# Layer 3 of a four-layer graph network: bursts of five units laid out in a table of eight bursts a batch

## Chip, cores and metric

One core of a Trainium2 chip (trn2). The metric is device time in microseconds (us) of one execution. The kernel before takes 2136.28 us, the median of three runs (2132.42 to 2140.51).

## The reference

Four graph layers over `x` of 16 batches, 1024 nodes and 64 features, with one adjacency matrix of 1024 x 1024 for all. After each layer `x = layernorm(x + layer(x))`. The change touches the last layer alone:

```python
# layer 3: four heads of dimension 64, then one outer attention
mask = adj + eye(N) > 0
h = einsum('bnc,hdc->bhnd', x, Wh)
scores = where(mask, h @ h^T, -1e16)          # per batch and head, 1024 x 1024
out_h = softmax(scores) @ h + bh
z = leaky_relu(concatenate(out_h), 0.2)       # 1024 x 256
h2 = z @ Wo^T
out2 = softmax(where(mask, h2 @ h2^T, -1e16)) @ h2 + bo
z2 = leaky_relu(out2, 0.2)
out = layernorm(z2) * gamma + beta
x = layernorm(x + out)
```

## The kernel before, in words

**Work and tiles.** P = 128 partitions, C = 8 blocks of nodes, HALF = 512 columns. Layers 0 to 2 come first; the loops of layer 3 stand at lines 1606 to 1732. In layer 3 the four heads of a batch are two pairs (n = 0, 1), two heads of 64 rows in one tile of 128 partitions. The work comes in **units**. A head unit takes one block k of source nodes and one half h of the target columns, for both heads of a pair: scores on PE (L1273, four MATMULs in the trace) into a PSUM tile `s` of 128 x 1024; exp on ACT (L1277) into an SBUF tile `e`, with a per-pair bias `shift`; the 0/1 mask on DVE (L1278); and the product with the values (L1285, four MATMULs), which adds up over the eight blocks in a PSUM bank. That is 32 units a batch. An outer unit (`head_out`, 8 a batch) is the same with h2: L1370, L1375, the mask into a second tile `me` (L1377), the product L1397; the row sums are made by one more DVE instruction, `add_up` (L1388), from the unmasked `e`.

**Small tasks.** When a half of a pair is complete, ACT copies it (L1292), and `project(q)` (L1294 to L1316) multiplies it with `wb`: eight matmuls (L1302), then on DVE a copy of the sums, a reciprocal, two multiplications and `leaky` into `z`. `z_T` transposes z, `h_2T` makes h2 (PE, ACT copy and square, two DVE copies), `h_2v` its transposed values. `shift_of` (L1205) makes the bias: matmuls of squares with ones into a PSUM tile `pn`, a maximum on DVE (`top`, L1214), an all-reduce over the partitions on POOL (L1216), and `below` (L1221), a DVE instruction that is put into the list `soon`. `prep_x`, `prep_h`, `prep_sq`, `prep_v` prepare the next pair of batches. An outer result then goes through `gather`, `layer`, `mean`, `centre`, `scale`, `affine`, `residual`, `mean`, `centre`, `scale`, `finish`, nearly all on DVE; `scale` also puts a root (two small ACT instructions) into `soon`, and the root puts its three DVE steps there.

**Order.** `tc.manual_schedule` keeps PE, ACT, DVE and POOL each in the order in which the program writes. `run` (L1708) takes the units of all batches from one queue, three to a burst. Of a burst it writes: `catch_up` (all of `soon`); of each unit scores, exp and mask; the tasks in `mids`; `drain`, the products of the burst before; the tasks in `slots`; the `add_up`s. So PE makes the scores of one burst before the products of the last one. Tasks are placed by batch and by the unit's position in it (0 to 39, the outer units of the batch before at 18, 21, ...).

**Buffers.** All small tasks and scores of layer 3 share three PSUM tiles of two banks (tag `s`), taken in turn. The tiles `e`, `me` and the second load of the adjacency (`nodes_adj`, a DMA on SP's queue and a conversion on DVE) share nine SBUF tiles (tag `e`).

Of the kernel before, what the change touches and what calls it, by code (L numbers as in the profile page):

```python
# [578 lines left out]
def fast_path(  # L579
# [87 lines left out]

    soon = []
    in_order = {getattr(mybir.EngineType, e) for e in ("PE", "Activation", "DVE", "Pool")}
# [43 lines left out]
    def normalizing(y, sq, late):  # L713
# [15 lines left out]
        def scale():  # L729
            vs = small.tile([P, n], F32, tag="ln_vs", name="ln_vs")  # L730
            nc.vector.tensor_reduce(vs, sq, AX.X, ALU.add)
            ve = small.tile([P, n], F32, tag="ln_ve", name="ln_ve")
            nc.vector.tensor_scalar(ve, vs, 1.0 / D, LN_EPS, ALU.mult, ALU.add)
            rstd = small.tile([P, n], F32, tag="ln_rstd", name="ln_rstd")
            if late:
                nc.gpsimd.tensor_tensor(rstd, ve, neg_half, ALU.pow)
                return rstd
            root, step = inverse_root(rstd, ve)

            def first():  # L740
                root()
                soon.append(step)

            soon.append(first)
            return rstd
# [444 lines left out]
    def nodes_adj(c):  # L1190
        a_sb = l3.tile([P, N], I32, tag="e", name=f"adj3_{c}", bufs=9)
        nc.sync.dma_start(a_sb, adj_v[c])

        def convert():
            nc.vector.tensor_scalar(
                aN[:, c, :].rearrange("p (k q) -> p k q", q=P), a_sb.rearrange("p (q k) -> p k q", k=C),
                0.0, None, ALU.is_gt,
            )
            own = aN[:, c, c * P : (c + 1) * P]
            nc.vector.tensor_tensor(own, own, ident16, ALU.max)  # L1200

        return convert
# [61 lines left out]
    def heads(b, n):  # L1264
        held = {}

        def scores(k, h):
# [3 lines left out]
            for i in range(2):  # L1271
# [3 lines left out]
                )  # L1275
            e = l3.tile([P, 2, HALF], F32, tag="e", name="e", bufs=9)
            nc.scalar.activation(e, s, AF.Exp, bias=shifts[b, n])  # L1277
            nc.vector.tensor_tensor(e, e, bc_mid(aT[:, k, cols], 2), ALU.mult)  # L1278
            return e

        def product(k, h, e):
# [7 lines left out]
            if k == C - 1:  # L1289
                if h == 0:  # L1290
                    held["y"] = l3.tile([P, N], F32, tag="y", name=f"yT_{b}_{n}")
                nc.scalar.copy(held["y"][:, h * HALF : (h + 1) * HALF], held[h])  # L1292

        def project(q):  # L1294
# [5 lines left out]
            for j in range(CH):  # L1300
                c = q * CH + j
                nc.tensor.matmul(  # L1302
                    o[:, j // 2, j % 2, :], held["y"][:, c * P : (c + 1) * P], wb[:, n, :], start=True, stop=True,
                )
# [5 lines left out]
            for i in range(2):  # L1310
# [6 lines left out]

        units = [(lambda k=k, h=h: scores(k, h), lambda e, k=k, h=h: product(k, h, e), None)
                 for h in range(2) for k in range(C)]
        return units, project  # L1320


    def prep_out(b):
# [28 lines left out]
        def h_2v():  # L1352
            v = l3.tile([P, C, D], F32, tag="h2v", name=f"h2v_{b}", bufs=1)
            pt = one_bank("ph2v").rearrange("p (c d) -> p c d", c=C)
            for c in range(C):
                nc.tensor.transpose(pt[:, c, :], hTs[b][0][:D, c // CH, c % CH * P : (c % CH + 1) * P], ident[:D, :D])
            nc.vector.tensor_copy(v, pt)  # L1357
            vals["out", b] = v
# [3 lines left out]
    def head_out(b):  # L1362
        held = {}

        def scores(k):
            s = ps_s.tile([P, 2, HALF], F32, tag="s", name="s")
            hT = hTs[b][0]
            for i in range(2):
# [4 lines left out]
                )  # L1373
            e = l3.tile([P, 2, HALF], F32, tag="e", name="e", bufs=9)
            nc.scalar.activation(e, s, AF.Exp, bias=shifts[b])  # L1375
            m = l3.tile([P, 2, HALF], F32, tag="e", name="me", bufs=9)
            nc.vector.tensor_tensor(  # L1377
                m, e, aT[:, k, :].rearrange("p (i q) -> p i q", i=2), ALU.mult
            )
            return e, m  # L1380

        def unit(k):
            held[k], m = scores(k)
            return m

        def add_up(k):
            junk = l3.tile([P, N], BF16, tag="junk", name="junk", bufs=1)
            nc.vector.scalar_tensor_tensor(  # L1388
                junk, held.pop(k).rearrange("p i q -> p (i q)"), 1.0, aN[:, k, :], ALU.mult, ALU.mult,
                accum_out=sums[:, b, H, k : k + 1],  # L1390
            )

# [55 lines left out]
        def finish():  # L1448
# [4 lines left out]
        units = [  # L1453
            (lambda k=k: unit(k), lambda e, k=k: product(k, e), lambda k=k: add_up(k)) for k in range(C)
        ]
# [148 lines left out]


    slots, mids = {}, {}
    work = [[heads(b, n) for n in range(NP)] for b in range(B)]
    outs = [(prep_out(b), head_out(b)) for b in range(B)]
    BURST = 3
    LAST = 40  # L1610
    E = B - 1

    def at(b, p, task, where=slots):
        where.setdefault((b, p), []).append(task)

    for c in range(C):
        convert = {}
        at(0, 2 * c, lambda c=c, convert=convert: convert.update(go=nodes_adj(c)))
        at(0, 2 * c + 5, lambda convert=convert: convert["go"]())
    for b in range(B):  # L1620
# [6 lines left out]
        ends = outs[b][1][1]  # L1627
        if b < E:
            places = [13, 22, 26, 33, LAST + 4, LAST + 7, LAST + 10, LAST + 13, LAST + 14]

            end = (41, 46, 49, 55) if b < E - 2 else (29, 31, 33, 39)
            places += [2 * LAST + p for p in (6, 8, 10, 11, 14, 23, 25, *end)]
        else:
            places = [13, 22, 26, 35, *[LAST - 1] * 5, *[LAST + 8] * 11]
        if b == E - 1:
            places[9:] = [LAST + 38, *[LAST + 39] * 4, *[2 * LAST + p for p in (3, 3, 3, 3, 3, 8)]]
        for task, p in zip(chain + ends, places):
            t = min(p // LAST, max(E - b, 0))
            at(b + t, p - t * LAST, task)


    ended = slots[E, LAST - 1]
    slots[E, LAST - 1] = [ended[i] for i in (5, 0, 1, 6, 2, 3, 7, 8, 9, 4)]
    ahead = []
    for b in range(0, B, 2):
        for t, p, task, where in (
            (-1, 16, lambda b=b: prep_x(b), slots),
            (-1, 20, lambda b=b: prep_h(b, 0, 0), mids), (-1, 23, lambda b=b: prep_sq(b, 0, 0), slots),
            (-1, 26, lambda b=b: prep_h(b, 0, 1), mids), (-1, 29, lambda b=b: prep_sq(b, 0, 1), slots),
            (-1, 25, lambda b=b: prep_v(b), slots),  # L1650
            (-1, 32, lambda b=b: shift_of((b, 0), hTs[b, 0][1]), slots),
            (-1, 36, lambda b=b: shift_of((b + 1, 0), hTs[b + 1, 0][1]), slots),
            (0, 2, lambda b=b: prep_h(b, 1, 0), mids), (0, 3, lambda b=b: prep_sq(b, 1, 0), slots),
            (0, 5, lambda b=b: prep_h(b, 1, 1), mids), (0, 8, lambda b=b: prep_sq(b, 1, 1), slots),
            (0, 11, lambda b=b: shift_of((b, 1), hTs[b, 1][1]), slots),
            (0, 20, lambda b=b: shift_of((b + 1, 1), hTs[b + 1, 1][1]), slots),
            (0, 19, lambda b=b: prep_v(b + 1), slots),
        ):
            if b + t < 0:
                ahead.append(task)  # L1660
            else:
                at(b + t, p, task, where)

    with tc.tile_pool(name="ps_g", bufs=1, space=bass.MemoryType.PSUM, reuse_waits="tile") as ps_g, tc.tile_pool(
# [13 lines left out]
        ending = gat_layer(later["w2"], "l2", True, extra, first, 5, True)  # L1678
    for p, task in zip((1, 4, 7, 10, 14, 16), ending):
        at(0, p, task)  # L1680

# [16 lines left out]

    queue = []
    for b in range(B):  # L1700
        units = work[b][0][0] + work[b][1][0]
        outer = outs[b - 1][1][0] if b else [None] * C
        for i, unit in enumerate(outer):
            units.insert(18 + (3 if b < E else 2) * i, unit)
        queue += [(b, p, unit) for p, unit in enumerate(units)]
    last = [(E, LAST + p, unit) for p, unit in enumerate(outs[E][1][0])]

    def run(queue):  # L1708
        while queue:
            burst = []  # L1710
            while queue and sum(unit is not None for _, _, unit in burst) < BURST:
                burst.append(queue.pop(0))
            catch_up()
            made = [(unit[1], unit[0]()) for _, _, unit in burst if unit]
            for b, p, _ in burst:
                tasks(mids, b, p)
            drain()
            waiting.extend(lambda product=product, e=e: product(e) for product, e in made)
            if not queue:
                drain()  # L1720
            for b, p, _ in burst:
                tasks(slots, b, p)
            for _, _, unit in burst:
                if unit and unit[2]:
                    unit[2]()

    with tc.manual_schedule(engines=in_order):
        run(queue)
        run(last)
        for task in [catch_up, *slots[E, LAST + 8]]:  # L1730
            task()
            while soon:
                catch_up()

# [72 lines left out]
```

## Time and profile before

| | us |
|---|---|
| median of three runs | 2136.28 |
| the profiled execution | 2138.12 |
| its span, first to last instruction | 2136.3 |
| PE busy | 2017.2 (94%) |
| DVE busy | 1851.9 (87%) |
| ACT busy | 1227.7 (57%) |
| POOL busy | 51.2 (2%) |
| first L1273 matmul (layer 3 begins) | 695.6 |
| head exps L1277, 512 of 1.11 us | 542.5 |
| head masks L1278, 512 of 1.22 us | 602.7 |
| outer masks L1377, 128 of 1.22 us | 155.9 |
| outer sums L1388, 128 of 1.22 us | 156.0 |

The span runs from the first to the last instruction; 1.8 us of the execution lie outside it. Busy time is the union of an engine's instructions. Matmuls overlap, so their ends run into the next one: the distance of two starts tells what a matmul costs, not its duration. The same holds in a smaller measure for DVE and ACT, where the mean of 1.22 us a mask goes with 1.135 us from start to start when masks follow each other. In rows of instructions in order of time, "x12" merges neighbours of one kind, and the bracket behind gives the idle time before them and what ended it.

### The profile page before, as it was taken

How to read it: one execution, taken by the hardware profiler on the slowest of the kernel's cores; microseconds unless marked ns; L12 is line 12 of the kernel's file. 1: busy time of each engine (PE TensorE's matmuls, PEld its weight loads, DVE VectorE, ACT ScalarE, POOL GpSimd, SP SyncE). 2: the span in 40 equal slices, each digit the busy share in tenths (PEclk: the TensorE clock that was granted, in tenths of full speed). 3: DMA queues.
4: the chain of work that ended last, by engine and by line, in shares of the span. 5: the costliest groups of instructions: out<-in, count | busy, mean ns of one | idle time of the engine just before them, and what ended most of it. 6: DMA issues, size and time to landing. Idle time of an engine off the chain costs nothing.

```text
span 2136.3 us, 26123 instructions
## 1 busy us (share of the span) xinstructions
PE 2017.2 (94%) x10065; PEld 841.9 (39%) x10065; DVE 1851.9 (87%) x3224; ACT 1227.7 (57%) x1965; POOL 51.2 (2%) x77
## 2 busy tenths in 40 slices
PE   7999979999887999999999999999999999999993
PEld 3333347763332333333334333333333333333331
DVE  5888879989999868798898898889888889889997
ACT  4445556645555756556665655655655665565541
POOL 0000000000000000000000000000000000000001
PEclk9999989989999999999999999999999999999997
DMA  6000000000000100000000000000000000000000
GB/s 165 1 1 1 1 1 1 1 1 1 0 1 30 50 1 1 1 1 6 6 1 6 1 6 6 1 6 1 6 6 1 6 1 6 6 1 6 6 5 12
DMA packets 23654, 18.89 MB, mean 9 GB/s; under 512 B 19361, under 2 KB 19426, under 8 KB 23522
## 3 DMA queue, kind: packets, MB, share of 16 engines
q1 hardware_dynamic: 23218, 17.11, 2.8%
q8 instruction: 81, 1.33, 0.3%
q14 instruction: 51, 0.42, 0.1%
q10 hardware_dynamic: 304, 0.03, 0.0%
HBM read 12.95 MB, written 4.19 MB: 8 GB/s over the span
## 4 chain that ended last, share of the span: by engine, by line
PE 69%; DVE 25%; ACT 3%; issue 1%; DMA 0%; POOL 0%; SPq 0%; POOLq 0%; DVEq 0%; ACTq 0%
PE y L1285 18%; PE s L1273 17%; DVE e L964 7%; PE y_l L976 6%; PE s L1370 5%; PE y L1397 4%; DVE e L1278 4%; PE u_l L987 3%; PE po L1302 3%; PE po L1557 3%; ACT e L1277 1%; PE pg L944 1%; DVE r L1566 1%; PE pzT L1331 1%; PE ps L910 1%
## 5 line engine op out<-in xcount | busy, mean ns | idle before, releaser
L1277 ACT ACTIVATE e<-s,shift 128x1024 f32<-128x1024 f32 x512 | 542.5, 1111 | 243.1 <-PE s L1273 237.6
L1278 DVE TENSOR_TENSOR e<-e,aT 128x1024 f32<-128x1024 f32 x512 | 602.7, 1221 | 87.3 <-ACT e L1277 85.3
L1273 PE MATMUL s<-hT 64*128 64x512 f32 x2048 | 509.6, 611 | 15.5 <-DVE top L1214 8.6
L1285 PE MATMUL y<-e,vals 128*64 128x512 f32 x2048 | 490.6, 601 | 3.2 <-ACT yT L1292 1.3
L964 DVE SCALAR_TENSOR_TENSOR e<-G_l,q,aT 128x1024 f32<-128x1024 f32 x256 | 320.0, 1280 | 20.9 <-ACT G_l L945 12.8
L976 PE MATMUL y_l<-e,vals_l 128*64 128x512 f32 x1024 | 271.3, 637 | 26.5 <-DVE e L964 25.8
L1273 PEld LDWEIGHTS s<-hT 64*128 64x128 f32 x2048 | 182.4, 186 | 256.1 <-issue 170.8
L1285 PEld LDWEIGHTS y<-e,vals 128*64 128x64 f32 x2048 | 131.0, 136 | 330.6 <-issue 258.0
L1375 ACT ACTIVATE e<-s,shift 128x1024 f32<-128x1024 f32 x128 | 141.6, 1112 | 85.2 <-PE s L1370 75.0
L1377 DVE TENSOR_TENSOR me<-e,aT 128x1024 f32<-128x1024 f32 x128 | 155.9, 1221 | 16.8 <-ACT e L1375 16.5
L1388 DVE SCALAR_TENSOR_TENSOR junk<-e,aN 128x1024 bf16<-128x1024 f32 x128 | 156.0, 1219 | 0.2
L1397 PE MATMUL y<-me,h2v 128*64 128x512 f32 x512 | 135.3, 609 | 10.5 <-DVE me L1377 10.4
L1370 PE MATMUL s<-h2T 64*128 64x512 f32 x512 | 136.3, 610 | 4.6 <-DVE h2v L1357 4.4
L976 PEld LDWEIGHTS y_l<-e,vals_l 128*64 128x64 f32 x1024 | 60.7, 139 | 169.8 <-issue 57.1
L1557 PE MATMUL po<-hi,aR 128*128 128x512 f32 x256 | 102.8, 401 | 2.8 <-ACT hi L1542 1.1
L775 ACT ACTIVATE x<-m,bn_shift,bn_rstd 128x64 f32<-128x64 f32 x256 | 88.5, 430 | 23.2 <-DVE bn_shift L766 23.2
L1557 PE MATMUL po<-lo,aR 128*128 128x512 f32 x256 | 100.2, 392 | 0.0
L1332 ACT COPY zT<-pzT 128x1024 f32<-128x1024 f32 x32 | 32.4, 1013 | 78.4 <-PE pzT L1331 78.4
L1302 PEld LDWEIGHTS po<-wb,yT 128*128 128x128 f32 x512 | 62.0, 190 | 34.0 <-issue 21.1
L1302 PE MATMUL po<-wb,yT 128*128 128x130 f32 x512 | 73.8, 287 | 1.3 <-ACT e L1277 1.2
L1370 PEld LDWEIGHTS s<-h2T 64*128 64x128 f32 x512 | 46.6, 186 | 63.7 <-issue 41.3
L987 PE MATMUL u_l<-e,only 128*32 128x512 f32 x512 | 70.3, 605 | 0.0
(214 smaller groups left out, 1980.8 us busy)
## 6 DMA issues: line engine op xcount, KB each, us to landing
adj<-in_adj_dram SPq DMA_DIRECT2D x16, 512.0 KB, 4.5
x<-in_x_dram SPq DMA_DIRECT2D x16, 256.0 KB, 4.9
out_dram<-res SPq DMA_DIRECT2D x16, 256.0 KB, 2.0
wl<-in_L_gnn_Wh_dram SPq DMA_DIRECT2D x2, 64.0 KB, 3.3
wo<-in_L_gnn_Wo_dram SPq DMA_DIRECT2D x1, 64.0 KB, 3.0
l_wd<-in_L_gnn_W_dram ACTq DMA_DIRECT2D x2, 16.0 KB, 4.9
l_wd<-in_L_gnn_W_dram SPq DMA_DIRECT2D x2, 16.0 KB, 2.1
bo<-in_L_gnn_bo_dram SPq DMA_DIRECT2D x1, 32.0 KB, 3.0
```

The lines of the kernel that those rows point to most:

```text
L964: nc.vector.scalar_tensor_tensor(e, G[b - b % 2][:, b % 2, :], pq[b - b % 2][1][:, k, b % 2 : b % 2 + 1], aT[:, k, :], ALU.max, ALU.mult,)
L976: nc.tensor.matmul(held["y"][h * D : (h + 1) * D, :], vals[b][:, k, :], e[:, h * HALF : (h + 1) * HALF], start=(k == 0), stop=(k == C - 1),)
L1273: nc.tensor.matmul(s[:, i, :], hT[rows, k * P : (k + 1) * P], hT[rows, cols], start=True, stop=True)
L1277: nc.scalar.activation(e, s, AF.Exp, bias=shifts[b, n])
L1278: nc.vector.tensor_tensor(e, e, bc_mid(aT[:, k, cols], 2), ALU.mult)
L1285: nc.tensor.matmul(held[h][i * D : (i + 1) * D, :], vals[b][:, k, :], e[:, i, :], start=(k == 0), stop=(k == C - 1),)
L1302: nc.tensor.matmul(o[:, j // 2, j % 2, :], held["y"][:, c * P : (c + 1) * P], wb[:, n, :], start=True, stop=True,)
L1370: nc.tensor.matmul(s[:, i, :], hT[rows, (i + k // CH) % 2, k % CH * P : (k % CH + 1) * P], hT[rows, 0, :], start=True, stop=True,)
L1377: nc.vector.tensor_tensor(m, e, aT[:, k, :].rearrange("p (i q) -> p i q", i=2), ALU.mult)
L1388: nc.vector.scalar_tensor_tensor(junk, held.pop(k).rearrange("p i q -> p (i q)"), 1.0, aN[:, k, :], ALU.mult, ALU.mult, accum_out=sums[:, ...
L1397: nc.tensor.matmul(held["o"][h * D : (h + 1) * D, :], vals["out", b][:, k, :], e[:, h, :], start=(k == 0), stop=(k == C - 1),)
L1557: nc.tensor.matmul(po.rearrange("p q k f -> p (q k f)"), aR[:, k, ic * P : (ic + 1) * P], e[:, k].rearrange("p q k f -> p (q k f)"), start ...
```

## The change

Bursts take five units instead of three, and a table says what goes with each of eight bursts a batch: bursts 0 to 3 hold five head units, bursts 4 to 7 three head units with two outer units of the batch before between them (positions 1 and 3). Tasks are placed by burst; most of those that stood in `slots`, behind the products, now stand in `mids`, ahead of them. Masks leave the scores and become a step of their own, written behind `mids` and the products, ahead of `slots`. Roots get a list of their own, run behind `mids`. An outer tile is summed first and then masked in place, except in the last batch, where the mask still goes to a second tile ahead of the sum; `junk` takes the buffer of `v3`. Each half has its own tile `y`, in one buffer, which `project` reads. The copy of h2v moves from DVE to ACT. There are eleven tiles `e` instead of nine. The eight conversions of the second adjacency load come one burst after their loads.

```diff
-    soon = []
+    soon, roots = [], []
...
-            soon.append(first)
+            roots.append(first)
...
-        a_sb = l3.tile([P, N], I32, tag="e", name=f"adj3_{c}", bufs=9)
+        a_sb = l3.tile([P, N], I32, tag="e", name=f"adj3_{c}", bufs=11)
...
-            e = l3.tile([P, 2, HALF], F32, tag="e", name="e", bufs=9)
+            e = l3.tile([P, 2, HALF], F32, tag="e", name="e", bufs=11)
             nc.scalar.activation(e, s, AF.Exp, bias=shifts[b, n])
-            nc.vector.tensor_tensor(e, e, bc_mid(aT[:, k, cols], 2), ALU.mult)
+            return e
+
+        def mask(k, h, e):
+            nc.vector.tensor_tensor(e, e, bc_mid(aT[:, k, h * HALF : (h + 1) * HALF], 2), ALU.mult)
             return e
...
-                if h == 0:
-                    held["y"] = l3.tile([P, N], F32, tag="y", name=f"yT_{b}_{n}")
-                nc.scalar.copy(held["y"][:, h * HALF : (h + 1) * HALF], held[h])
+                held["y"] = l3.tile([P, HALF], F32, tag="y", name=f"yT_{b}_{n}_{h}", bufs=1)
+                nc.scalar.copy(held["y"], held[h])
...
-                    o[:, j // 2, j % 2, :], held["y"][:, c * P : (c + 1) * P], wb[:, n, :], start=True, stop=True,
+                    o[:, j // 2, j % 2, :], held["y"][:, j * P : (j + 1) * P], wb[:, n, :], start=True, stop=True,
...
-            nc.vector.tensor_copy(v, pt)
+            nc.scalar.copy(v, pt)
             vals["out", b] = v
...
-            m = l3.tile([P, 2, HALF], F32, tag="e", name="me", bufs=9)
-            nc.vector.tensor_tensor(
-                m, e, aT[:, k, :].rearrange("p (i q) -> p i q", i=2), ALU.mult
+            return e
+
+        def add_up(k, e):
+            junk = l3.tile([P, CH, P], F32, tag="v3", name="junk", bufs=1)
+            nc.vector.scalar_tensor_tensor(
+                junk.rearrange("p c q -> p (c q)").bitcast(BF16), e.rearrange("p i q -> p (i q)"), 1.0, aN[:, k, :],
+                ALU.mult, ALU.mult, accum_out=sums[:, b, H, k : k + 1],
             )
...
+        def mask(k, e):
+            m = e
+            if b < B - 1:
+                add_up(k, e)
+            else:
+                m = l3.tile([P, 2, HALF], F32, tag="e", name="me", bufs=11)
+            nc.vector.tensor_tensor(m, e, aT[:, k, :].rearrange("p (i q) -> p i q", i=2), ALU.mult)
+            if b == B - 1:
+                add_up(k, e)
             return m
...
-    BURST = 3
-    LAST = 40
+    BURSTS = 8
...
+        places = [(3, mids), (5, mids), (8, mids), (7, mids), (9, mids), (9, slots), (10, mids), (11, mids), (12, mids)]
+        places += [(18, mids), *((j, slots) for j in (18, 19, 19, 20, 22, 24, 24, 24, 25, 28))]
+        if b == E - 2:
+            places[9:] = [(17, mids), *((j, slots) for j in (17, 17, 18, 18, 20, 20, 21, 22, 22, 24))]
+        elif b == E - 1:
+            places[9:] = [(j, slots) for j in (15, 15, 15, 15, 15, 16, 16, 16, 16, 16, 18)]
+        elif b == E:
+            places[2] = 7, mids
+            places[4:] = [(j, slots) for j in [7] * 5 + [10] * 11]
+        for task, (j, where) in zip(chain + ends, places):
+            t = min(j // BURSTS, E - b)
+            at(b + t, j - t * BURSTS, task, where)
...
+            (-1, 3, lambda b=b: prep_x(b), mids),
+            (-1, 4, lambda b=b: prep_h(b, 0, 0), mids), (-1, 4, lambda b=b: prep_sq(b, 0, 0), mids),
+            (-1, 5, lambda b=b: prep_h(b, 0, 1), mids), (-1, 5, lambda b=b: prep_sq(b, 0, 1), mids),
+            (-1, 6, lambda b=b: prep_v(b), slots),
+            (-1, 6, lambda b=b: shift_of((b, 0), hTs[b, 0][1]), mids),
+            (-1, 7, lambda b=b: shift_of((b + 1, 0), hTs[b + 1, 0][1]), mids),
+            (0, 0, lambda b=b: prep_h(b, 1, 0), mids), (0, 0, lambda b=b: prep_sq(b, 1, 0), mids),
+            (0, 1, lambda b=b: prep_h(b, 1, 1), mids), (0, 1, lambda b=b: prep_sq(b, 1, 1), mids),
+            (0, 2, lambda b=b: shift_of((b, 1), hTs[b, 1][1]), mids),
+            (0, 4, lambda b=b: shift_of((b + 1, 1), hTs[b + 1, 1][1]), mids),
+            (0, 6, lambda b=b: prep_v(b + 1), slots),
...
+        outer = outs[b - 1][1][0] if b else []
+        for j in range(BURSTS):
+            n = 5 if j < 4 else 3
+            burst, units = units[:n], units[n:]
+            if j >= 4:
+                for i, unit in enumerate(outer[2 * (j - 4) : 2 * (j - 3)]):
+                    burst.insert(1 + 2 * i, unit)
+            plan.append((b, j, burst))
+    units = outs[E][1][0]
+    last = [(E, BURSTS, units[:5]), (E, BURSTS + 1, units[5:])]
+
+    def run(plan):
+        for b, j, burst in plan:
             catch_up()
-            made = [(unit[1], unit[0]()) for _, _, unit in burst if unit]
-            for b, p, _ in burst:
-                tasks(mids, b, p)
+            made = [(unit, unit[0]()) for unit in burst]
+            tasks(mids, b, j)
+            while roots:
+                roots.pop(0)()
             drain()
+            made = [(product, mask(e)) for (_, mask, product), e in made]
             waiting.extend(lambda product=product, e=e: product(e) for product, e in made)
-            if not queue:
+            if (b, j, burst) == plan[-1]:
                 drain()
-            for b, p, _ in burst:
-                tasks(slots, b, p)
-            for _, _, unit in burst:
-                if unit and unit[2]:
-                    unit[2]()
+            tasks(slots, b, j)
```

In `places` the first nine entries are, in order, the projections of pair 0's halves, z_T(0), the projections of pair 1's halves, z_T(1), h_2T, the outer shift, h_2v; the other eleven are gather to finish. A place of 8 or more lies in a later batch: 11 is burst 3 of the next one.

## The prediction

> **What bounds the kernel now.** I read the page first, then its chain, then the time order of layer 3.
>
> ```profile
> span 2136.3 us, 26123 instructions
> ...
> PE 2017.2 (94%) x10065; PEld 841.9 (39%) x10065; DVE 1851.9 (87%) x3224; ACT 1227.7 (57%) x1965; POOL 51.2 (2%) x77
> ...
> DVE  5888879989999868798898898889888889889997
> ...
> PEclk9999989989999999999999999999999999999997
> ...
> PE 69%; DVE 25%; ACT 3%; issue 1%; DMA 0%; POOL 0%; SPq 0%; POOLq 0%; DVEq 0%; ACTq 0%
> ```
>
> PE carries 69% of the chain, DVE 25%; DMA nothing. Layer 3 runs from the first L1273 matmul at 695.6 us to the end. The busy time by stretches says how tight it is there (columns: stretch, its length, then busy us of PE, PEld, DVE, ACT, POOL, and the granted clock). The last of these three rows is six batches of layer 3:
>
> ```profile
> 506.00:510.49 4.49, 1.93 (x10) 0.41 (x8) 4.35 (x19) 1.04 (x4) 1.24 (x1) 1.00 0.00 0
> 510.49:513.91 3.42, 3.42 (x12) 1.82 (x10) 3.32 (x7) 2.37 (x11) 0.00 (x0) 0.50 0.01 2
> ...
> 887.07:1412.48 525.41, 516.86 (x2521) 199.81 (x2520) 460.12 (x687) 319.53 (x378) 11.23 (x18) 1.00 0.01 3
> ```
>
> 525.41 / 6 = 87.6 us a batch. PE idles (525.41 - 516.86) / 6 = 1.4, DVE works 460.12 / 6 = 76.7: PE bounds layer 3, with DVE close behind. Next, PE alone in time order; a start minus the start before is what a group cost:
>
> ```profile
> 1225.15 2.85 PE L1273 MATMUL s<-hT 64*128 64x512 f32 x12
> 1227.93 2.79 PE L1285 MATMUL y<-e,vals 128*64 128x512 f32 x12
> 1230.66 0.35 PE L1210 MATMUL pn<-pair_ones,hsq 128*128 128x2 bf16 x8
> ```
>
> Three units' scores cost 1227.93 - 1225.15 = 2.78, three products 1230.66 - 1227.93 = 2.73. Between units of one kind the step is 0.86 (outer scores at 1007.50, the next head's at 1008.36). So a burst of any size pays 2.78 - 3 x 0.86 + 2.73 - 3 x 0.86 = 0.35 us to turn PE between tile shapes.
>
> Last, DVE in time order where a shift is made: its maximum (top), a projection, a root's three steps, the shift (L1221), then masks, strictly one after the other:
>
> ```profile
> 2018.23 0.69 DVE L727 TENSOR_TENSOR m<-v 128x512 f32<-128x512 f32 x1
> 2018.84 0.16 DVE L1214 TENSOR_REDUCE top<-pn 128x1 f32<-128x8 f32 x1
> ...
> 2020.14 0.69 DVE L781 SCALAR_TENSOR_TENSOR z<-v 128x512 f32<-128x512 f32 x1
> ...
> 2021.23 0.14 DVE L1221 TENSOR_SCALAR shift<-gtop 128x1 f32<-128x1 f32 x1
> 2021.30 3.48 DVE L1278 TENSOR_TENSOR e<-e,aT 128x1024 f32<-128x1024 f32 x3
> ```
>
> A shift becomes ready only when DVE has come through everything written ahead of it. Today it is wanted two or three bursts later and costs nothing: the one exp wait on L1221 in the whole layer is 2.8 us, in the last batch.
>
> **Longer bursts.** 632 units in threes and the last 8 make 214 bursts; 16 x 8 + 2 = 130 remain. 84 x 0.35 = 29 us, about 1.9 a batch. PE's 1.4 idle a batch stems from shift maxima, h2v copies on DVE and score buffers; I let all of it go. 15 x 3.3 = **-50**.
>
> **Masks behind the small tasks.** This turns DVE's order round: the projection, the h2T copies and the maximum stand ahead of a burst's masks, and wait for PE, which makes them only after five scores. I follow burst 3 of an odd batch from its first score (time 0). Rows: a mask 1.135 (three in 3.49), an exp 1.01 (three in 3.12), the first exp 1.17 after the first score (1210.12, 1211.29).
> - PE: scores to 5 x 0.86 + 0.2 = 4.5; shift matmuls to 4.8; the projection needs the fourth exp's PSUM tile, free at 1.17 + 4 x 1.01 + 0.14 = 5.35, and ends at 6.4; prep_x to 7.4 (1.0); five products of the burst before, 4.35, to 11.75. There burst 4 starts.
> - DVE: projection data at 6.6, its five instructions 1.84, to 8.4; five masks 5.7, to 14.1; mean and centre of an older batch (0.69 + 0.17 + 0.69 + 0.69, less overlap, 2.15), to 16.3.
> So DVE enters burst 4 some **4.5 us late**. For the products this is covered: burst 3's masks are wanted from 4.5 us on into burst 4, the last 3.4 later. With that cover gone each us late is a us of PE.
>
> **What is not covered is the shift.** The outer shift's maximum is taken in burst 3 and its L1221 stands at the head of burst 4, where the second unit is already an outer one. Its exp could run at 1.17 + 1.01 = 2.2; it gets its shift at 4.5 + 0.2 and ends at 5.9. ACT is in order, there are three score tiles, and the fifth score needs the tile of the second exp: PE stands from 3.5 to 5.9, **2.4 us**. In even batches the shift of the second head pair does the same from burst 2 to unit 16 in burst 3 (gather, h2T and its ACT copy come first, DVE is late by 4.4): 2.0 us, and then DVE is a further 0.9 late in burst 4. 8 odd batches x 2.4 + 7 even x (2.0 + 2.4 + 0.9) = **+56**.
>
> Small tasks ahead of the products also wait for score tiles: the projection of burst 3 (0.5) and h2T of burst 2 (0.3), about 0.9 a batch: **+14**.
>
> **Outer tiles masked in place.** The sum (1.22 + 0.08, 1.26 start to start) now precedes its mask, so an outer product waits 2.4 instead of 1.1 a unit; 3 x 1.135 + 2 x 2.4 = 8.2 us a mixed burst, hidden by the 8 us that PE spends on scores and small tasks before those products are due. Without that cover 60 bursts x 2.5 = 150 us: an upper end that DVE's 76.7 of 87.6 excludes. At the end nothing covers it: the last mixed burst's 8.2 us replaces two masks (2.3): **+6**.
>
> **At nothing.** Projection by halves: the same eight matmuls and one 0.59 copy each, each half read before the next is written. junk in v3's buffer: both on DVE. h2v to ACT: 0.68 less on DVE in burst 4, 0.59 on ACT, which is 57% busy. Roots move behind the small tasks: ACT waits there for DVE's variance, due 4-6 us into the burst, with its exps running to 6.4; then a y copy would be late. The second adjacency loads on SP's queue (4.5 us) have a burst of 9 us; eleven tiles hold two bursts of five plus one. Each is within 0 to 0.5 a batch, so -2 to +7 in all; I take 0.
>
> **The clock.** PE in time order, just ahead of the stretch that ran at 0.50:
>
> ```profile
> 509.20 2.09 PE L976 MATMUL y_l<-e,vals_l 128*64 128x512 f32 x6 [2.54 <-DVE e L964]
> ```
>
> PE stood 2.54 us, and the 3.42 us from 510.49 on were granted half the clock. In the six batches of layer 3 PE's longest wait is 1.2 us, and the row shows 1.00. The new waits of 2.0 to 3.3 lie around that 2.5. Each cold stretch costs 3.42 / 2 = 1.7; if two in three of the 15 outer waits bring one, 17, of which a third comes back because DVE is less late after it: **+11** (bounds 0 and 22 x 1.7 = 37).
> The Trainium skill, "TensorE: Matmul & The Clock Gate", Part 1, says that the clock halves after at least one idle window of about 3.4 us; by that none of these waits would be long enough and the sum would be 11 lower. The row at 509.20 differs, and the measurement decides.
>
> **Sum**: -50 + 56 + 14 + 6 + 11 = +37 against the profiled execution's 2138.1 us (span 2136.3), which stands 0.1% over the median of 2136.28. On the median: 2136 + 37 = **2173 us**.
>
> **Rivals.**
> 1. *The waits come, the clock stays*: 2173 - 11 = 2162. For it: the waits of 2.0 to 2.4 lie under 2.54.
> 2. *Faster: DVE is not late.* If DVE enters bursts 3 and 4 less than 2.1 us late, exp ends (2.1 + 0.2 + 1.2) before the fifth score wants its tile at 3.5, and the 56 and 11 are gone: 2106. The point that decides is lateness at burst start, 4.5 by my rows. For it: 10.9 us of DVE are free a batch. Against: DVE cannot spend them while it waits for PE's small tasks.
> 3. *Half late* (3.0 to 3.8 us): each wait is 1.5 to 0.7 shorter, and the clock stays: 2162 - 22 x 1.5 = 2129 to 2162 - 22 x 0.7 = 2147, within measurement of no change. For and against it stands the same lateness.
>
> **Chances.** Forecast 0.62, rival 1 0.15, rival 2 0.12, rival 3 0.11. Half a per cent, 11 us, is about what a measurement of this kernel can tell from no change. Slower: 0.62 + 0.15 and a little of rival 3, 0.79; same 0.09; faster 0.12. The range takes in the forecast with its clock bound (2162 to 2190), rival 1 and rival 3's upper half, and leaves out rival 2: 2140 to 2192.
>
> **What would show it.** Right: exp L1277 or L1375 waiting on DVE L1221, some 22 times, 2 to 3 us each, in the waits; PE idle 2 to 3 us inside a score group; batches of 89 to 90 us; clock rows at 0.50 in layer 3. PE turns fewer by 84. Wrong: DVE idle before masks rather than before projections; no waits on L1221; batches under 85. My sum fails most easily in DVE's lateness: a us more or less there moves it by 22.

## The result

The changed kernel takes **2194.93 us** (median of four runs, 2193.32 to 2196.95) against 2134.79 for the kernel before (four runs, 2132.42 to 2140.51): a ratio of 1.028, 95% interval 1.026 to 1.030. That is slower, as forecast, and just past the upper end of the range. The profiled execution took 2194.18 us with a span of 2192.3, 56 us more than before's span, where the sum had 37.

From the page after: the span, the busy times, TensorE's granted clock by slices, the chain, and three groups of the costliest, with their idle time and what ended it.

```profile
span 2192.3 us, 26200 instructions
...
PE 2031.2 (93%) x10065; PEld 865.8 (39%) x10065; DVE 1843.2 (84%) x3208; ACT 1230.9 (56%) x1981; POOL 64.4 (3%) x77
...
PEclk9999989989999999999999999999999999999997
...
PE 46%; DVE 42%; ACT 9%; issue 3%; SPq 0%; DMA 0%; POOL 0%; POOLq 0%; ACTq 0%; DVEq 0%
...
L1282 DVE TENSOR_TENSOR e<-e,aT 128x1024 f32<-128x1024 f32 x512 | 601.2, 1219 | 1.9 <-ACT e L1278 1.8
L1274 PE MATMUL s<-hT 64*128 64x512 f32 x2048 | 503.7, 610 | 44.5 <-ACT e L1379 31.3
...
L1308 DVE COPY sums<-po 128x8 f32<-128x8 f32 x64 | 10.9, 170 | 111.0 <-PE po L1304 111.0
```

In the kernel before, DVE's idle time ahead of the masks, from its page, and ahead of the projections' sums, from its waits (us in total, times, longest), was:

```profile
L1278 DVE TENSOR_TENSOR e<-e,aT 128x1024 f32<-128x1024 f32 x512 | 602.7, 1221 | 87.3 <-ACT e L1277 85.3
...
DVE sums L1306 <- PE po L1302: 52.0, 54, 1.7
```

DVE is busy for less time than before (1843 against 1852) and yet its share of the chain rises from 25% to 42%: it does no more, it comes later. It no longer idles ahead of masks (87.3 us before, 1.9 now) but ahead of projections (52.0 before, 111.0 now). PE now idles 31.3 us inside the scores for the outer exp. The waits say for what that exp stood (columns: who waited for whom, us in total, times, longest):

```profile
DVE sums L1308 <- PE po L1304: 111.0, 49, 6.0
...
ACT e L1379 <- DVE shift L1222: 33.9, 14, 3.4
...
PE s L1274 <- ACT e L1379: 31.3, 14, 3.1
...
ACT e L1278 <- DVE ln_step L708: 11.6, 6, 1.9
```

Burst 4 of an odd batch, PE, DVE and ACT taken together from the time order (start, length, engine, group, idle before):

```profile
1162.88 1.13 PE L1274 MATMUL s<-hT 64*128 64x512 f32 x4
...
1165.56 1.02 PE L1374 MATMUL s<-h2T 64*128 64x512 f32 x4
...
1167.45 0.15 DVE L1222 TENSOR_SCALAR shift<-gtop 128x1 f32<-128x1 f32 x1
...
1167.69 1.11 ACT L1379 ACTIVATE e<-s,shift 128x1024 f32<-128x1024 f32 x1 [2.52 <-DVE shift L1222]
...
1168.86 1.13 PE L1274 MATMUL s<-hT 64*128 64x512 f32 x4 [2.27 <-ACT e L1379]
```

The burst starts at 1162.88, the shift comes 4.57 us later (forecast 4.5), and the fifth scores start 5.98 us after the burst (forecast 5.9). In even batches the same happens twice, in burst 3 as well. There the view puts the head exp's wait down to `ln_step` (the last row of the waits), which DVE starts 0.07 us behind the shift; what that exp reads is the shift. The kernel before has one such wait in the whole layer, 2.8 us in the last batch.

The steady part of layer 3, from the first scores of batch 0 to those of batch 15, took 1290.2 us before (695.6 to 1985.8) and 1344.5 after (694.1 to 2038.6): **+54.3**. The end, from there on, went from 150.5 to 153.8, and the layers ahead from 695.6 to 694.1. From batch 8 on, even batches take 94.6 us and odd ones 89.6 or 89.7, against a mean of 1290.2 / 15 = 86.0 before.

What the sum hardly held is the clock. In layer 3 the records show TensorE at 0.50 for 75 us between 697 and 2140, where before had none from 699 to 2104; the page's slices, in tenths, do not tell the two apart. Two stretches of an even batch, one after the other (columns: stretch, length, busy us of PE, PEld, DVE, ACT, POOL, granted clock, DMA share, GB/s):

```profile
1430.59:1434.00 3.41, 1.65 (x10) 0.81 (x11) 0.41 (x3) 3.41 (x4) 0.35 (x1) 0.99 0.00 0
1434.00:1437.41 3.41, 3.41 (x14) 1.94 (x14) 1.75 (x6) 0.62 (x1) 0.00 (x0) 0.51 0.02 5
```

PE worked 1.65 us of the first stretch, broken by waits of 1.70 us (1.06 of it inside the stretch) and 0.70 us, and ran the whole of the next one at half speed.

### The profile page after: what moved, and what is told of

Same layout as the page of the kernel before. It is cut to its first block, busy times and chain, and to the rows that moved or that the text cites. A ratio compares the mean times of both kernels' runs of the same rounds, so it can differ in the third digit from the quotient of the medians.

```text
span 2192.3 us, 26200 instructions
## 1 busy us (share of the span) xinstructions
PE 2031.2 (93%) x10065; PEld 865.8 (39%) x10065; DVE 1843.2 (84%) x3208; ACT 1230.9 (56%) x1981; POOL 64.4 (3%) x77
## 4 chain that ended last, share of the span: by engine, by line
PE 46%; DVE 42%; ACT 9%; issue 3%; SPq 0%; DMA 0%; POOL 0%; POOLq 0%; ACTq 0%; DVEq 0%
DVE e L1282 14%; PE y L1289 10%; PE s L1274 9%; DVE e L965 6%; PE y_l L977 6%; ACT e L1278 5%; DVE junk L1384 3%; PE u_l L988 3%; PE po L1564 3%; PE po L1304 3%; DVE e L1395 3%; PE y L1404 2%; PE s L1374 2%; ACT e L1379 2%; DVE v L1314 2%
## 5 line engine op out<-in xcount | busy, mean ns | idle before, releaser
L1282 DVE TENSOR_TENSOR e<-e,aT 128x1024 f32<-128x1024 f32 x512 | 601.2, 1219 | 1.9 <-ACT e L1278 1.8
L1274 PE MATMUL s<-hT 64*128 64x512 f32 x2048 | 503.7, 610 | 44.5 <-ACT e L1379 31.3
L1289 PE MATMUL y<-e,vals 128*64 128x512 f32 x2048 | 510.3, 622 | 5.6 <-ACT yT L1295 4.3
L1289 PEld LDWEIGHTS y<-e,vals 128*64 128x64 f32 x2048 | 140.0, 142 | 291.2 <-issue 195.6
L1379 ACT ACTIVATE e<-s,shift 128x1024 f32<-128x1024 f32 x128 | 142.1, 1116 | 36.4 <-DVE shift L1222 33.9
L1395 DVE TENSOR_TENSOR e<-e,aT 128x1024 f32<-128x1024 f32 x120 | 147.0, 1225 | 6.4
L1374 PE MATMUL s<-h2T 64*128 64x512 f32 x512 | 131.6, 596 | 0.0
L1404 PE MATMUL y<-e,h2v 128*64 128x512 f32 x480 | 123.4, 593 | 2.6 <-DVE e L1395 2.6
L1308 DVE COPY sums<-po 128x8 f32<-128x8 f32 x64 | 10.9, 170 | 111.0 <-PE po L1304 111.0
L1217 POOL PARTITION_ALL_REDUCE gtop<-top x48 | 41.6, 867 | 1451.3 <-DVE top L1215 1448.7
```

The source lines that it names most:

```text
L1274: nc.tensor.matmul(s[:, i, :], hT[rows, k * P : (k + 1) * P], hT[rows, cols], start=True, stop=True)
L1282: nc.vector.tensor_tensor(e, e, bc_mid(aT[:, k, h * HALF : (h + 1) * HALF], 2), ALU.mult)
L1289: nc.tensor.matmul(held[h][i * D : (i + 1) * D, :], vals[b][:, k, :], e[:, i, :], start=(k == 0), stop=(k == C - 1),)
L1374: nc.tensor.matmul(s[:, i, :], hT[rows, (i + k // CH) % 2, k % CH * P : (k % CH + 1) * P], hT[rows, 0, :], start=True, stop=True,)
L1395: nc.vector.tensor_tensor(m, e, aT[:, k, :].rearrange("p (i q) -> p i q", i=2), ALU.mult)
```

## Experiments

The theory after the result: DVE reaches the shift late, the shift is wanted at once, PE stands, and the standing brings half clock. Rival B: the longer bursts themselves, or the sums ahead of the outer masks, cost the time. Rival C: the waits cost it and the clock adds little. All ratios are to the kernel before, run on the same chip.

### e1: the shift ahead of the masks

```diff
-        soon.append(below)
+        belows.append(below)
...
             drain()
+            while belows:
+                belows.pop(0)()
             made = [(product, mask(e)) for (_, mask, product), e in made]
```

> The shift's negation (L1222) is written just ahead of the masks of the burst that makes its maximum, not at the head of the next burst; nothing else changes. Theory (the exps wait for a shift that DVE reaches late, and the waits bring cold clock): the 8 x 2.3 + 7 x (2.5 + 1.7 + 0.7) = 52 us of waits and the 75 us at half clock (37 us of work) both go, so 2195 - 52 - 37 = 2106, faster than the kernel before; no exp waits on L1222 and no rows at 0.50 in layer 3. Rival B (the longer bursts themselves, or the sums standing ahead of the outer masks, cost it): above 2180. Rival C (the waits cost, the clock adds little): 2195 - 52 = 2143.

Measured: 2108.34 us, ratio **0.988** (0.985 to 0.991). One instruction per shift, moved up by the masks of a burst, turns 2.8% slower into 1.2% faster; a second series (e9 below) gives 0.990. The time order of DVE in an even batch, burst 3, and PE and ACT in the burst 4 that follows:

```profile
1393.90 0.15 DVE L1222 TENSOR_SCALAR shift<-gtop 128x1 f32<-128x1 f32 x1
1393.97 5.75 DVE L1282 TENSOR_TENSOR e<-e,aT 128x1024 f32<-128x1024 f32 x5
...
1398.59 1.11 ACT L1379 ACTIVATE e<-s,shift 128x1024 f32<-128x1024 f32 x1
...
1399.64 0.68 DVE L722 TENSOR_REDUCE ln_sum<-v 128x8 f32<-128x512 f32 x1
...
1399.93 1.02 PE L1274 MATMUL s<-hT 64*128 64x512 f32 x4
```

Burst 4 starts at 1396.39. DVE still enters it late: its masks run to 1399.72 and a mean and a centre follow. But the shift has been there since 1394, the outer exp starts without a wait, and so do the fifth scores. The steady part takes 1263.3 us, 81 less than after's, every batch from the third on 85.7 or 86.0, and no exp from batch 0 to 15's start waits on L1222. Rivals B and C are out in their strong form: with DVE still late, the kernel is faster than the one before.

### e2: masks first again

```diff
             made = [(unit, unit[0]()) for unit in burst]
+            made = [(product, mask(e)) for (_, mask, product), e in made]
             tasks(mids, b, j)
...
             drain()
-            made = [(product, mask(e)) for (_, mask, product), e in made]
```

> The masks stand right behind the scores again, ahead of the small tasks: only this part of the change is undone. Theory: DVE enters the next burst about 1 us late instead of 4.5, the shift is there before its exp or within 0.3 us, waits and cold clock go, less a few us because the small tasks' results now wait behind five masks: 2106 to 2130. Rival B: above 2180. Rival C: 2143 to 2165.

Measured: 2128.92 us, ratio 0.997 (0.995 to 0.999). The exps' waits on the shift are gone here too, but 20 us of e1's gain are missing, 16 of them in the steady part (1279.2 against 1263.3). PE and DVE where these went, in time order:

```profile
1364.65 1.13 PE L1274 MATMUL s<-hT 64*128 64x512 f32 x4
1365.40 0.16 DVE L1308 COPY sums<-po 128x8 f32<-128x8 f32 x1
1365.60 0.20 DVE L1310 RECIPROCAL rt<-sums 128x8 f32<-128x8 f32 x1
...
1365.84 0.75 DVE L1314 TENSOR_TENSOR v<-po,rt 128x256 f32<-128x256 f32 x2
...
1366.74 3.70 PE L1274 MATMUL s<-hT 64*128 64x512 f32 x16 [0.96 <-DVE v L1314]
```

The projection was ready early (PE made it from 1358.94 on), but DVE read it only behind the masks and sums of five units, and until then it kept one of the three score tiles. That is what masks behind the small tasks are good for with long bursts: they give the tile back sooner.

### e3 and e5: the waits kept, the clock held up

```diff
+    def filler(b):
+        t = ps_h.tile([P, HALF], F32, tag="acc0", name="filler")
+        hT = hTs[b, 1][0]
+        for _ in range(2):
+            nc.tensor.matmul(t, hT[:D, :P], hT[:D, :HALF], start=True, stop=True)
...
-            made = [(unit, unit[0]()) for unit in burst]
+            made = []
+            for i, unit in enumerate(burst):
+                if i == 4 and b and (j == 4 or j == 3 and b % 2 == 0):
+                    filler(b)
+                made.append((unit, unit[0]()))
```

> Two matmuls whose result nobody reads (0.86 us each, on the scores' operands) are added just ahead of the fifth scores of burst 4 of every batch but the first, and of burst 3 of even batches: they fill 1.7 us of the wait and take none away. Theory (cold clock is a cost of its own): the waits for the shift stay at about their size counted with the fillers, the rows at 0.50 go, and with them up to 37 us: 2158 to 2170. Rival C: 2190 to 2196, fillers make no difference.

Measured: 2181.74 us, ratio 1.022 (1.020 to 1.025): between the two expectations. 27 us at 0.50 stayed, all of them behind burst 4 of even batches, where PE still idled 1.43 us behind its fillers; six of the seven such batches had a row. So e5 takes three fillers there:

```diff
-                    filler(b)
+                    filler(b, 3 if j == 4 and b % 2 == 0 else 2)
```

> As e3, with three fillers instead of two in burst 4 of even batches, whose wait was the longest. In e3 the one steady even batch without a row at 0.50 took 91.2 us, the odd ones 88.6, against 94.6 and 89.6 with the change. Theory (the clock's net cost is what a fully warm run saves: 7 x 3.4 + 6 x 1.0 = 30 at most, some 25 with the early batches, which had fewer cold rows): even batches 91.2, odd 88.6, no rows at 0.50 in the steady part of layer 3, 2165 to 2172. Rival C (the clock adds about 11, as forecast, and e3 has shown all of it): 2180 to 2185.

Measured: 2170.62 us, ratio 1.015 (1.012 to 1.018). Six batches each of after (6 to 11), e1 and e5 (3 to 8), in that order:

```profile
1208.87:1759.71 550.84, 524.31 (x2522) 210.66 (x2521) 458.19 (x685) 320.86 (x384) 16.22 (x18) 0.97 0.01 4
```

```profile
921.10:1436.10 515.00, 506.68 (x2524) 205.65 (x2522) 457.54 (x685) 319.58 (x384) 6.34 (x18) 1.00 0.01 4
```

```profile
935.30:1474.70 539.40, 527.48 (x2564) 212.77 (x2562) 458.03 (x685) 320.34 (x384) 16.20 (x18) 1.00 0.01 4
```

e5's PE does more matmuls (2564 against 2522), at full clock, and the six batches are 11.4 us shorter than after's. Even batches take 91.2 and odd ones 88.6, and the outer exps' waits on the shift are no shorter (40.0 us against 33.9): work that nobody reads makes the kernel 1.3 points faster. In e5, in the batches followed in time order (7 to 9), the fillers end 0.56 us or more before the scores may start in burst 4, so they lengthen nothing there; from 697 us on the steady part holds one row at 0.50, of 3.4 us, in batch 14. Rival C is out: the clock's net cost is 1344.5 - 1321.8 = 22.7 us in the steady part.

### e4: the outer units one place later

```diff
-                    burst.insert(1 + 2 * i, unit)
+                    burst.insert((2 if j == 4 else 1) + 2 * i, unit)
```

> In burst 4 the two outer units stand third and fifth instead of second and fourth. Theory: the first outer exp is wanted one exp (1.0 us) later and the fifth scores no longer need its tile; the wait in burst 4 becomes one of about 1.4 us at the first small task, so 15 x 0.9 = 13 us of waits go, and the cold stretches of the odd batches (some 24 us at 0.50, 12 of work) with them: 2165 to 2172. Rival C: 2182. Rival B: 2195, no change.

Measured: 2163.96 us, ratio 1.014 (1.011 to 1.017), 1 us under what the theory had. The exps' waits on the shift fall from 33.9 to 23.8 us. PE waits 1.41 us ahead of h2v in an undisturbed odd batch, and such a batch takes 87.6 us. Of the six odd batches from 3 to 13 one was followed by a row at 0.50; in after four were. In all the steady part had 20 us at 0.50 where after had 75, a larger fall than the theory's 24: in six of the seven even batches PE still waits 2.28 us in burst 4, but two of them had a row behind it, where in after all seven had. That part of the gain was not foreseen, and its cause is not shown.

### e6: masks ahead of the sums, on top of e1

```diff
-            m = e
-            if b < B - 1:
-                add_up(k, e)
-            else:
-                m = l3.tile([P, 2, HALF], F32, tag="e", name="me", bufs=11)
+            m = l3.tile([P, 2, HALF], F32, tag="e", name="me", bufs=11)
             nc.vector.tensor_tensor(m, e, aT[:, k, :].rearrange("p (i q) -> p i q", i=2), ALU.mult)
-            if b == B - 1:
-                add_up(k, e)
+            add_up(k, e)
```

> On top of e1: outer masks go into a tile of their own and stand ahead of the sum in every batch, as they do in the last one; masking in place is undone. Theory: the sums ahead of the outer masks are hidden by PE's scores and small tasks except at the end, so the steady part stays within 3 us of e1 and the tail gains 1 to 3: 2103 to 2109 with e1 at 2108. Rival B (the in-place order costs a wait per mixed burst): 2085 to 2095.

Measured: 2111.89 us, ratio 0.988 (0.986 to 0.990), no different from e1. The steady part is 1263.6 against 1263.3: the order of sum and mask is hidden. The end takes 152.8, no less than e1's 152.2, so it does not explain the end either.

### e7: masks written behind `mids` and the products, in the kernel before

```diff
             tasks(mids, b, p)
             drain()
+            made = [(product, mask()) for product, mask in made]
             waiting.extend(lambda product=product, e=e: product(e) for product, e in made)
```

(The masks leave `scores` for this; the bursts of three and all positions stay.)

> The kernel before, bursts of three as they are, with one thing of the change: the masks stand behind the small tasks and the products of the burst before. Theory: a shift is wanted two or three bursts after its maximum there, so no exp waits on it and no cold rows come from that; DVE's lateness in a burst of three can reach the products, which are wanted only 2.8 us plus the small tasks later: 2136 to 2165, and what it adds stands at products, not at exps. Rival (masks behind the small tasks cost the same wherever they stand, the bursts have no part in it): 2190 and exps waiting on L1221.

Measured: 2136.92 us, ratio **1.0005** (0.999 to 1.002). Six batches of it, columns as above:

```profile
933.60:1459.00 525.40, 516.83 (x2524) 199.77 (x2521) 461.02 (x691) 319.81 (x378) 11.25 (x18) 1.00 0.01 4
```

525.40 us for six batches, PE 516.83: what before takes, because it comes to the same program. In the kernel before, DVE's small tasks stand in `slots`, and the masks, though written later, still come ahead of `slots`. The two traces hold the same instructions in the same order on PE, DVE, ACT and POOL (all 3224 of DVE's). So e7 did not put a mask behind a small task, and it says nothing for the theory or its rival; whether that order costs anything in bursts of three stays open.

### e8: h2v back on DVE, on top of e1

```diff
-            nc.scalar.copy(v, pt)
+            nc.vector.tensor_copy(v, pt)
```

> On top of e1: the h2v copy goes back to DVE. Forecast counted its move at nothing: within 3 us of e1's 2108. Rival (DVE decides in burst 4, and 0.68 a batch there is seen): 2113 to 2120.

Measured: 2113.39 us, ratio 0.990 (0.988 to 0.992), which does not stand apart from e1's. Its steady part, 1263.1 us, is e1's: the move is worth nothing.

### e9 and e10: what is left

> e1 once more, to settle its ratio: 0.988 of the kernel before, 2105 to 2112. If the waits were all that kept the longer bursts from paying, this is what they pay.

Measured: 2112.32 us, ratio 0.990 (0.988 to 0.992). The same kernel as e1, and the same answer.

```diff
-            tasks(mids, b, j)
+            for i, task in enumerate(mids.get((b, j), [])):
+                if i == 1 and j in (3, 4):
+                    waiting.pop(0)()
+                task()
```

> e1, and in bursts 3 and 4 one product of the burst before is put between the first small task of PE and the second. e1's PE still idles 0.6 us a batch ahead of the projection in burst 3 and 0.3 ahead of the second small task in burst 4, each waiting for a score tile. Theory (these idles are the small tasks' waits for score tiles that the forecast put at 0.9 a batch): they go, less two more turns of PE at some 0.1 to 0.3 each: 0.3 to 0.7 a batch, 5 to 10 us under e1. Rival (the idle only moves to the products or the next burst): within 3 us of e1.

Measured: 2102.53 us, ratio **0.984** (0.981 to 0.986), the fastest of all. PE in burst 3, in time order: a product fills the time in which the projection had waited for its tile.

```profile
1391.92 0.25 PE L1211 MATMUL pn<-pair_ones,h2sq 128*128 128x2 bf16 x4
1392.10 1.08 PE L1289 MATMUL y<-e,vals 128*64 128x512 f32 x4
1393.11 1.16 PE L1304 MATMUL po<-wb,yT 128*128 128x130 f32 x8
```

And six of its batches:

```profile
926.70:1437.30 510.60, 507.72 (x2524) 204.38 (x2522) 457.47 (x685) 319.63 (x384) 6.31 (x18) 1.00 0.01 4
```

PE idles (510.60 - 507.72) / 6 = 0.48 us a batch, against (515.00 - 506.68) / 6 = 1.39 in e1; the steady part is 1253.0, 10.3 less than e1's.

## Why the prediction was right and where it was not

The mechanism, its places and the direction were right. The runs split the span's +56 by the same terms:

| term | forecast | measured | read from |
|---|---|---|---|
| bursts, with small tasks' waits | -50 + 14 = -36 | -27 | steady part of e1 less before: 1263.3 - 1290.2 |
| waits for the shift | +56 | +58 | e5 less e1: 1321.8 - 1263.3 |
| clock | +11 | +23 | after less e5: 1344.5 - 1321.8 |
| end | +6 | +3 | 153.8 - 150.5 |
| layers ahead | 0 | -1.5 | 694.1 - 695.6 |

**The waits (+56): right**, by batch, and in the total with some luck. Odd batches cost 88.6 - 86.0 = 2.6 in e5 against e1 (forecast 2.4), even ones 91.2 - 85.7 = 5.5 (forecast 2.0 + 2.4 + 0.9 = 5.3). "DVE enters burst 4 some 4.5 us late" met 4.57. But batch 1, counted with the odd ones, had no such wait and batch 15 one of 0.89 us; what made the total up again is 0.2 more in each of the others, 1.1 and 1.2 in batches 0 and 1, and some 1.7 from e5's one row at 0.50.

**The clock (+11): the step that failed**, and the largest share of the miss. The sum had "two in three of the 15 outer waits" bring one stretch of 3.42 us, about ten. There were 75 / 3.42, about 22: an odd batch brought one after its burst 4 in four cases of six, an even one two or three, because the wait in its burst 3 brought one too in five cases of seven, and because the half speed behind its burst 4 lasted two stretches in six of seven (why two is open). I had set the waits against a single idle of 2.54 us and overlooked that 1.70 and 0.70 close together do the same. At half speed the 75 us lose 37, the upper bound that I had written down and not taken. The range had not taken it either: 2162 + 37 is 2199, not the 2190 that it gives for the forecast with its clock bound. "A third comes back" held: of 37, 23 stayed, or some 24 with e5's one row.

**The bursts (-50): some 4 too high; the small tasks' waits (+14): 7 too low.** PE's busy time, which the turns are part of, fell by (516.86 - 506.68) / 6 = 1.70 a batch in e1 against the 1.9 counted, so 25 instead of 29 us. PE's idle of 1.43 a batch did go, as the forecast let it, but 1.39 came back at other places, ahead of the projection in burst 3 (0.61), behind h2v (0.3), ahead of h2T (0.21) and of products; 0.9 had been counted (of the two parts named there, 0.5 and 0.3, the sum is 0.8). Together 15 x (-1.70 - 1.43 + 1.39) = -26, near the -27 measured. e10 shows what most of these were: with a product in between they go.

**The end (+6)**: +3, and e6 shows that the order of sum and mask is not its cause. The long-burst kernels end in 152 to 156 us, those with bursts of three in 150.2 and 150.5, all of them with 20 us or more at half clock; the cause of the difference stays open.

**What was counted at nothing** held where it was tried: h2v on ACT (e8) and masking in place (e6). The roots' move, the projection by halves and the second adjacency loads were not tried one by one; e1 bounds them together with the rest at the -27.

**The rivals.** Rival 2 gave 2106 for a kernel whose shift waits and clock loss are gone, and that kernel, e1, took 2108 and in e9 2112; part of the nearness is luck, since the bursts gained 9 less and the end cost less than its sum has. But its point of decision, DVE less than 2.1 us late, was put wrongly: in e1 DVE is late and the gain comes all the same. What decides is when the shift is written against when it is wanted. Rival 1, the waits without the clock, was 2162; e5 put it at 2171. Rival 3 did not occur.

## What to carry to other kernels

When an engine's order is turned round, look for the small instruction that now stands behind the large ones and is wanted next: here a shift of 0.15 us behind five masks took away nearly 4% of the time, and long bursts with the shift early gained 1.2% (e1) or 1.0% (e9). Price a repeated wait of PE with its clock as well: look at the idle within each few microseconds and not only at the longest single gap, and take the upper bound when the wait returns every batch. A filler on PE tells the clock's share from the wait's. And an edit that moves a line of the program need not move an instruction (e7's did not): the trace tells.

## What the runs showed of the hardware

PE need not be idle for a whole stretch to lose its clock. In after, 1.65 us of work in 3.41, the idle broken in two, was followed by a half-speed stretch (the rows at 1430.59 and 1434.00), and one wait of 2.27 us in an odd batch by another, at 1171.1. Shorter waits could do it: those of 1.43 us in e3 were followed by a row in six of seven even batches, those of 1.41 us in e4 once in six odd batches, and e5's one row had no wait longer than 0.57 us in the 10 us ahead of it. Nor did the same wait always do it: the 2.27 us of after's odd batches were followed by a row in four of six, and 2.28 us in even batches of e4 in two of six. So the length of the wait alone does not decide; what else does is not shown.

The Trainium skill, "TensorE: Matmul & The Clock Gate", Part 1, in its table of the two states, asks for at least one idle window of about 3.4 us. In after no wait of PE on the outer exp was longer than 3.1 us, and the clock was halved for 75 us in all. The measurement decides.
